# Last layer of a four-layer network: the order of an iteration around VectorE, spreads in one group, mixing in ten steps on a PSUM bank of its own

## The chip, the cores and the metric

The kernel runs on one core of a Trainium2 chip. The metric is the device time of one execution in microseconds (us). The engines are TensorE (PE in the profile, its weight loads PEld), VectorE (DVE), ScalarE (ACT), GpSimd (POOL) and SyncE (SP, which here only issues transfers). Each works through its own queue of instructions, and they wait for one another by semaphores.

## The reference

Four layers work in turn on x, 16 batches of 256 tokens of 128 channels (float32). The change touches the last one. It normalises x, adds an attention scaled per batch by a gate, normalises again, and adds a gated mixing. The attention's sequence runs over the 16 batches: each of the 256 columns attends, for every one of 16 heads of 8 channels, from batch u to the batches 0 to u.

```python
def _L3_attn_ref(x, W_qkv, b_qkv, W_out, b_out):
    T, B, D = x.shape            # 16, 256, 128; H, Dh = 16, 8
    q, k, v = jnp.split(x @ W_qkv + b_qkv, 3, axis=-1)   # to_heads
    scores = jnp.einsum('bhqd,bhkd->bhqk', q, k) / jnp.sqrt(jnp.float32(Dh))
    scores = jnp.where(causal, scores, -jnp.inf)
    context = jnp.einsum('bhqk,bhkd->bhqd', jax.nn.softmax(scores, axis=-1), v)
    return context @ W_out + b_out

def _L3_ffn_ref(x, W_r, W_k, W_v, mu_r, mu_k):
    # x_prev: x one token earlier in its batch, 0 before the first
    xr = mu_r * x + (1.0 - mu_r) * x_prev
    xk = mu_k * x + (1.0 - mu_k) * x_prev
    r = jax.nn.sigmoid(xr @ W_r)
    return r * (jnp.square(jax.nn.relu(xk @ W_k)) @ W_v)

h = _layernorm(x) * (1 + ca) + sa
x = x + ga * _L3_attn_ref(h, ...)
h = _layernorm(x) * (1 + cb) + sb
x = x + gb * _L3_ffn_ref(h, ...)
```

## The kernel before

x lies in SBUF with the channels on the 128 partitions and the 4096 tokens as columns; a batch is 256 columns, a block (two batches) 512. The attention is not done as matrices of queries by keys. For batch u, VectorE multiplies the queries by the keys of all batches up to u, column by column; TensorE sums each head's 8 channels with a matrix of ones, and later spreads the 16 head weights back to 128 channels.

`layer3` (L2287) runs a ring of iterations u = 0 to 18 written out by hand. Iteration u works on four batches at once: u (products), w = u - 1 (softmax), z = u - 2 (weighted values) and a = u - 3 (output projection). The steps are:

- `queries(u)` (L2310): one matmul into the bank ps_q.
- `scores(u, c)` (L2314): VectorE, qk = (ps_q + bias) * keys, for the part c of the earlier batches. `parts` (L2306) makes one part of up to 8 batches, two from u = 8 on.
- `heads(u, c)` (L2323): 8 matmuls with 32 columns of weights, in the trace 16 rows, since a float32 matmul is two passes; the sums S lie in one bank of the pool behind `bank()`.
- `exps(w)` (L2339): VectorE's maximum (top) and subtraction (E), then ScalarE's exponential. `weights(w)` (L2348): VectorE's sum and reciprocal (tot), then the product on GpSimd (E<-E,tot).
- `spread(z, c, half)` (L2355): 4 matmuls (8 rows) into one of two double banks of ps_big. A half is 128 of the 256 tokens.
- `weighted(z, c, half)` (L2364): VectorE's product pv of the spread weights and the values; after the second half a tree of additions on GpSimd, which leaves one or two batches' worth for the projection. The last tree of batch 15 is on VectorE.
- `projected(a)` (L2383): matmuls with the output weights into a bank of `bank()`; `added(a)` (L2390): ScalarE's t (gate and bias), then x += t on GpSimd, and the start of a mixing.

Beside the ring there are generators in the list `sides`; `tick()` advances each by one step, up to its next yield. `keys3(blk)` (L2225) normalises a block and makes its keys and values: blocks 0 to 2 inside layer 2, 3 to 7 in the ring at u = 0, 2, 4, 6 and 8. `mixing3(b0, nb)` (L2239) is the second half of the layer for two batches after every odd one, and for batches 14 and 15 one at a time; it ends with the transfer of x to the output on SP. Both use `normed3` (L2205): the mean by a matmul, ln_xc = x - mean on VectorE, the square on ScalarE, its mean by a matmul, the logarithm and exponential on ScalarE, and the product on GpSimd. Layer 2 calls `keys3` and `normed3` too.

Inside the ring `strict_all` is set, so that every instruction of TensorE, VectorE, ScalarE and GpSimd stays in the order in which the program issues it. Nearly all of them go through the helpers at L219 (VectorE, ScalarE, GpSimd) and L265 (matmuls), and so have those lines in the profile; tiles tell them apart. PSUM has 8 banks: four for ps_big, one for ps_q, three in rotation for `bank()`, which serves heads, projections, keys and mixings (all ps_one in the profile).

## Time and profile before

| | us |
|---|---|
| median of 3 runs | 2811.61 (2802.94 to 2819.47) |
| the profiled execution | 2822.73 |
| its span, first to last instruction | 2821.0 |
| last layer's attention: first product qk (iteration 0) | at 2597.4 |
| first row of iteration 16 (top of batch 15) | at 2768.1 |
| last addition on GpSimd | 2815.3 to 2816.0 |

In the span TensorE is busy for 2574.2 us (91%), VectorE 1856.5 (66%), ScalarE 1590.8 (56%) and GpSimd 1255.8 (45%). The last layer takes about 224 us of the 2821.0; from 2597.35 to 2821.0 TensorE is busy for 171.8 us, VectorE 125.1, GpSimd 112.4 and ScalarE 93.2. These times come from one profiled execution. A row of the timeline gives the start, the length, the engine, the line, the operation with output and inputs, and in brackets how long the engine had been idle before it and what ended the wait. PEclk is the clock that was granted to TensorE, as a share of full speed.

### The profile page before, as it was taken

The page shows a single profiled execution, that of the slowest core. Times are in us where ns is not written, and L with a number is a line of the kernel's source. Part 1 is how long each engine was busy: PE and PEld are TensorE (multiplying, and loading weights), DVE is VectorE, ACT ScalarE, POOL GpSimd, SP SyncE. Part 2 cuts the span into 40 slices and gives each one's busy share as a digit, 9 for nine tenths or more (in the row PEclk, how much of TensorE's full clock was granted, in tenths as well). Part 3 has the DMA queues.
Part 4 walks back from the last instruction along what each step waited for, and adds up shares of the span by engine and source line. Part 5 has one row for each costly group of instructions (what it writes and reads, how often), then busy time and mean ns, then how long its engine had stood idle before and what let it go on. Part 6 is the DMA issues. An engine that isn't in the chain of part 4 may idle for free.

```text
span 2821.0 us, 49133 instructions
## 1 busy us (share of the span) xinstructions
PE 2574.2 (91%) x17190; PEld 1694.3 (60%) x17190; DVE 1856.5 (66%) x4449; ACT 1590.8 (56%) x4166; POOL 1255.8 (45%) x1105
## 2 busy tenths in 40 slices
PE   7999999989799999999999888889889999999886
PEld 4566566656588677777666545558645555443443
DVE  6777767787654467666666777773467885654664
ACT  4666666666544566666665466665435555532533
POOL 5767776876413553334444300142565442000555
PEclk9999999999999999999999999999989999999988
DMA  9240000000177200000000122327623231221000
GB/s 333 33 41 1 7 10 1 11 26 5 38 216 216 88 16 3 1 1 1 1 31 16 49 89 81 98 75 215 202 76 109 86 92 47 79 82 56 8 8 16
DMA packets 119286, 181.04 MB, mean 64 GB/s; under 512 B 18096, under 2 KB 81008, under 8 KB 116736
## 3 DMA queue, kind: packets, MB, share of 16 engines
q1 hardware_dynamic: 97360, 148.51, 18.4%
q0 software_dynamic: 8432, 17.31, 2.2%
q10 hardware_dynamic: 13248, 12.06, 1.2%
q8 instruction: 138, 2.26, 0.3%
q14 instruction: 108, 0.88, 0.1%
HBM read 120.38 MB, written 60.58 MB: 64 GB/s over the span
## 4 chain that ended last, share of the span: by engine, by line
PE 52%; DVE 21%; ACT 14%; POOL 5%; issue 5%; DMA 2%; SPq 1%; DVEq 0%; ACTq 0%; POOLq 0%
PE ps_one L265 24%; PE ps_big L265 8%; ACT E L219 8%; PE ps_one L268 6%; PE ps_out L265 4%; PE ps_hid L265 4%; PE ps_max L265 4%; DVE m L219 3%; POOL E L219 3%; DVE PT L219 3%; DVE r_t L219 2%; DVE sm_neg L219 2%; ACT r_sq L219 1%; PE ps_exp L265 1%; ACT ln_sq L219 1%
## 5 line engine op out<-in xcount | busy, mean ns | idle before, releaser
L219 POOL TENSOR_TENSOR E<-E,sm_inv 128x1024 f32<-128x1024 f32 (+1 forms) x246 | 412.8, 1688 | 505.1 <-DVE sm_inv L219 483.2
L219 ACT ACTIVATE E<-E,sm_neg 128x256 f32<-128x256 f32 x512 | 252.7, 495 | 194.6 <-DVE sm_neg L1210 194.6
L219 ACT ACTIVATE E<-ps_exp 128x1024 f32<-128x1024 f32 x246 | 226.1, 919 | 165.1 <-PE ps_exp L265 162.1
L219 DVE TENSOR_REDUCE m<-ps_max 128x4 f32<-128x1024 f32 x242 | 263.8, 1090 | 82.6 <-PE ps_max L265 81.2
L268 PEld LDWEIGHTS ps_one<-w_cst,E 128*128 128x128 f32 x1792 | 206.9, 144 | 146.1 <-POOL E L219 86.6
L219 ACT ACTIVATE E<-ps_big,sm_neg 128x128 f32<-128x128 f32 (+1 forms) x512 | 208.9, 422 | 138.1 <-DVE sm_neg L219 114.5
L268 PE MATMUL ps_one<-w_cst,E 128*128 128x128 f32 x1792 | 243.3, 281 | 47.6 <-POOL E L219 30.5
L219 POOL DMA_INDIRECT rows<-list_rows,l_i x128 | 127.8, 999 | 342.8 <-DVE inv L219 158.8
L265 PE MATMUL ps_big<-kT,qT 64*128 64x256 f32 (+1 forms) x2048 | 250.7, 374 | 0.0
L219 DVE COPY PT<-ps_one 128x512 f32<-128x512 f32 x320 | 202.5, 678 | 70.5 <-PE ps_one L268 70.1
L265 PE MATMUL ps_one<-PT,v 128*64 128x256 f32 (+1 forms) x2048 | 223.4, 360 | 3.9 <-ACT v L219 2.1
L265 PEld LDWEIGHTS ps_big<-kT,qT 64*128 64x128 f32 x2048 | 173.9, 189 | 50.9 <-issue 35.4
L219 POOL DMA_INDIRECT list_rows<-done,origin x128 | 122.9, 960 | 173.3 <-ACT s L1098 55.2
L1210 DVE CUSTOM_DVE_ANT_0 E<-ps_big,bias 128x256 f32<-128x256 f32 x512 | 181.6, 419 | 6.7 <-PE ps_big L265 4.8
L265 PEld LDWEIGHTS ps_one<-PT,v 128*64 128x64 f32 x2048 | 130.9, 137 | 82.1 <-DVE sm_neg L1210 17.2
L219 POOL TENSOR_TENSOR r_r<-r_r,r_t 128x512 f32<-128x512 f32 x128 | 163.9, 1280 | 25.8 <-DVE r_t L219 23.7
L265 PE MATMUL ps_max<-q,q 60*128 60x256 f32 (+3 forms) x1008 | 127.6, 331 | 47.6 <-DVE m L219 34.8
L219 DVE TENSOR_TENSOR r_r<-ps_rope,a_cw 128x512 f32<-128x512 f32 x128 | 88.2, 689 | 122.4 <-ACT r_sq L219 115.0
L265 PEld LDWEIGHTS ps_max<-q,q 60*128 60x128 f32 (+1 forms) x1008 | 78.6, 192 | 138.1 <-DVE m L219 74.8
L265 PE MATMUL ps_rope<-w_a_qkv,hb 128*128 128x512 f32 x256 | 139.6, 630 | 17.8 <-DVE sm_inv L219 10.8
L219 POOL TENSOR_TENSOR ln_xc<-ln_xc,ln_sq 128x512 f32<-128x512 f32 (+1 forms) x41 | 51.1, 1246 | 234.3 <-ACT ln_sq L219 234.2
L219 POOL TENSOR_SCALAR_AFFINE_SELECT E<-E 128x512 f32<-128x512 f32 x128 | 83.8, 655 | 157.6 <-ACT E L219 157.3
(354 smaller groups left out, 5838.7 us busy)
## 6 DMA issues: line engine op xcount, KB each, us to landing
q<-parts SPq DMA_DIRECT2D x256, 128.0 KB
rows<-zeros SPq DMA_DIRECT2D x8, 2048.0 KB
share<-comb_rows SPq DMA_DIRECT2D x128, 128.0 KB
parts<-parts SPq DMA_DIRECT2D x14, 1024.0 KB
list_w<-in_f_W SPq DMA_DIRECT2D x46, 257.0 KB
done<-l_o ACTq DMA_DIRECT2D x92, 128.0 KB
f_W<-in_f_W SPq DMA_DIRECT2D x27, 386.0 KB
f_room<-in_f_W SPq DMA_DIRECT2D x19, 386.0 KB
```

Of the source, the lines that this page charges most:

```text
L219: ins = f(*args, **kw)
L265: self.ordered(self.nc.tensor.matmul(out, lhsT, rhs, start=start, stop=stop, **kw))
L268: self.ordered(self.nc.tensor.transpose(out, in_, self.c("ident")))
L1210: nc.vector.tensor_tensor_reduce(e[:, i], S[:, i], bias[g][:, i, off : off + T], 1.0, BIG, ALU.add, ALU.min, neg[:, i : i + 1])
```

## The change

Six things change, all in the last layer.

1. The order in an iteration. Before: spreads of z's first part, exps, scores, then halves of weighted and spread in turn with heads, weights, projection and ticks. After: both halves of weighted z, exps, scores, both spreads of z's second part, tick 1, projection, heads, weights, addition, tick 2, both halves of weighted z's second part, scores of the second part, tick 3, both spreads of w's first part, heads of the second part, queries, tick 4. From iteration 16 on the projection and addition come after weighted's second part, and ticks 1 and 2 are called once more.
2. The two halves of a part's spread are issued together.
3. Keys and mixings in the ring take a single bank, ps_side, and `bank()` keeps two banks. A flag, `side_held`, makes the others let a tick pass while a step's sum waits there for VectorE in a later step. The product on GpSimd in normed3 waits for tick 1 or 2.
4. A mixing of two batches has ten steps. The k product (squared ReLU) comes before r (sigmoid).
5. Batches 14 and 15: the addition to x is one VectorE instruction on the projection's sum, and their bias is added to x by ScalarE at the end of iteration 15. Their mixings have fewer steps, and the product of the normalisation, k's ReLU and square, r's ReLU and additions, and the last addition to x are on VectorE. Batch 15's mixing uses `bank()`, and h1b for the sigmoid's logarithm.
6. The final ticks alternate between tick 1 and tick 2.

```diff
@@ -2202,86 +2202,121 @@
         m = self.mods[3]
         self.act.activation(dst, src, AF.Identity, bias=m[:, 3 * half, b : b + 1], scale=m[:, 3 * half + 1, b : b + 1])
 
-    def normed3(self, src, out):
+    def normed3(self, src, out, bank=None, quick=False):
 
         n = src.shape[-1]
-        ps = self.bank()[:, :n]
+        get = bank or self.bank
+        while bank and self.side_held:
+            yield
+        ps = get()[:, :n]
+        self.side_held = bool(bank)
         self.mm(ps, self.c("mean"), src)
         yield
         xc = self.ln.tile([P, BLK], F32, tag="ln_xc", name="ln_xc")[:, :n]
         self.dve.tensor_sub(xc, src, ps)
+        self.side_held = False
         sq = self.ln.tile([P, BLK], F32, tag="ln_sq", name="ln_sq")[:, :n]
         self.act.activation(sq, xc, AF.Square)
         yield
-        ps = self.bank()[:, :n]
+        while bank and self.side_held:
+            yield
+        ps = get()[:, :n]
         self.mm(ps, self.c("mean"), sq)
-        yield
+        if not bank:
+            yield
         self.act.activation(sq, ps, AF.Ln, bias=self.eps5)
         self.act.activation(sq, sq, AF.Exp, scale=-0.5)
-        self.gps.tensor_mul(xc, xc, sq)
+        if quick:
+            self.dve.tensor_mul(xc, xc, sq)
+        else:
+            if bank:
+                yield
+                while self.phase not in (1, 2):
+                    yield
+            self.gps.tensor_mul(xc, xc, sq)
         out.append(xc)
         yield
 
-    def keys3(self, blk):
+    def keys3(self, blk, bank=None):
 
         out = []
-        yield from self.normed3(self.x[:, blk * BLK : (blk + 1) * BLK], out)
+        yield from self.normed3(self.x[:, blk * BLK : (blk + 1) * BLK], out, bank)
         h = self.h3[blk] = self.l3.tile([P, BLK], F32, tag="h3", name="h3", bufs=3)
         for i in range(2):
             self.shifted(h[:, i * T : (i + 1) * T], out[0][:, i * T : (i + 1) * T], 2 * blk + i, 0)
         yield
         for n, (dst, k) in enumerate(((self.k3, "a3_bk"), (self.v3, "a3_bv"))):
-            ps = self.bank()
+            while bank and self.side_held:
+                yield
+            ps = (bank or self.bank)()
             self.mm(ps, self.w3[:, (n + 1) * P : (n + 2) * P], h)
-            yield
+            if not bank:
+                yield
             self.act.activation(dst[:, 2 * blk : 2 * blk + 2, :].rearrange("p b t -> p (b t)"), ps, AF.Identity, bias=self.v(k))
-
-    def mixing3(self, b0, nb):
+            if bank and n == 0:
+                yield
+
+    def mixing3(self, b0, nb, bank):
 
         two, W = self.two3, nb * T
+        quick = nb == 1
         x = self.x[:, b0 * T : (b0 + nb) * T]
-        if nb == 2:
-            yield
-            yield
-        out = []
-        yield from self.normed3(x, out)
-
         h = two.tile([P, 2, T + 1], F32, tag="h3f", name="h3f")
         self.gps.memset(h[:, :, 0:1], 0.0)
+        if not quick:
+            yield
+        out = []
+        yield from self.normed3(x, out, bank, quick)
         for i in range(nb):
             self.shifted(h[:, i, 1:], out[0][:, i * T : (i + 1) * T], b0 + i, 1)
         yield
 
         def mixed(n):
-            ps = self.bank()[:, :W]
+            ps = bank()[:, :W]
             o = ps.rearrange("p (b t) -> p b t", t=T)
             self.mm(o, self.mix[2 * n], h[:, :nb, 1:], start=True, stop=False)
             self.mm(o, self.mix[2 * n + 1], h[:, :nb, :T], start=False, stop=True)
             return ps
 
+        r = two.tile([P, BLK], F32, tag="r3", name="r3")[:, :W]
+        k = two.tile([P, BLK], F32, tag="kr3", name="kr3")[:, :W]
+        l = self.h1[:, :W] if b0 < B - 1 else self.h1b[:, :W]
+        while self.side_held:
+            yield
+        ps = mixed(1)
+        if quick:
+            self.dve.tensor_scalar(k, ps, 0.0, None, ALU.max)
+            self.dve.tensor_mul(k, k, k)
+        else:
+            self.act.activation(k, ps, AF.Relu)
+            self.act.activation(k, k, AF.Square)
+        yield
+        while self.side_held:
+            yield
         ps = mixed(0)
-        yield
-
-        r = two.tile([P, BLK], F32, tag="r3", name="r3")[:, :W]
-        l = self.h1[:, :W]
         self.act.activation(l, ps, AF.Abs)
-        self.act.activation(r, ps, AF.Relu, scale=-1.0)
+        if quick:
+            self.dve.tensor_scalar(r, ps, -1.0, 0.0, ALU.mult, ALU.max)
+        else:
+            self.act.activation(r, ps, AF.Relu, scale=-1.0)
         self.act.activation(l, l, AF.Exp, scale=-1.0)
         self.act.activation(l, l, AF.Ln, bias=self.one)
-        self.gps.tensor_add(r, r, l)
-        ps = mixed(1)
-        yield
-        k = two.tile([P, BLK], F32, tag="kr3", name="kr3")[:, :W]
-        self.act.activation(k, ps, AF.Relu)
-        self.act.activation(k, k, AF.Square)
+        (self.dve if quick else self.gps).tensor_add(r, r, l)
+        if not quick:
+            yield
+        while self.side_held:
+            yield
+        ps = bank()[:, :W]
+        self.side_held = not quick
+        self.mm(ps, self.wv3, k)
         self.act.activation(r, r, AF.Exp, scale=-1.0)
-        ps = self.bank()[:, :W]
-        self.mm(ps, self.wv3, k)
-        yield
+        if not quick:
+            yield
         for i in range(nb):
             c = slice(i * T, (i + 1) * T)
             self.dve.scalar_tensor_tensor(r[:, c], ps[:, c], self.mods[3][:, 5, b0 + i : b0 + i + 1], r[:, c], ALU.mult, ALU.mult)
-        self.gps.tensor_add(x, x, r)
+        self.side_held = False
+        (self.dve if quick else self.gps).tensor_add(x, x, r)
         self.nc.sync.dma_start(out=self.out[:, b0 * T : (b0 + nb) * T], in_=x)
 
     def layer3(self):
@@ -2290,13 +2325,20 @@
         with ExitStack() as ctx:
             self.ps_big = self.pool("ps_big", 2, PSUM, ctx=ctx)
             self.ps_q = self.pool("ps_q", 1, PSUM, ctx=ctx)
-            self.ps_one = self.pool("ps_three", 3, PSUM, ctx=ctx)
+            self.ps_one = self.pool("ps_three", 2, PSUM, ctx=ctx)
+            ps_side = self.pool("ps_side", 1, PSUM, ctx=ctx)
+            self.side_held, self.phase = False, 0
             two = self.two3 = self.ln = self.pool("a3_two", 2, ctx=ctx)
             C = 32
             U = [{} for _ in range(B)]
             sides = []
 
-            def tick():
+            def side():
+                ps = ps_side.tile([P, BLK], F32, tag="side", name="ps_side")
+                return ps
+
+            def tick(phase=0):
+                self.phase = phase
                 for g in list(sides):
                     try:
                         next(g)
@@ -2388,16 +2430,18 @@
                     self.mm(d["A"], self.wo3, p, start=k == 0, stop=k == len(P_) - 1)
 
             def added(u):
-                t = two.tile([P, T], F32, tag="t3", name="t3")
-                self.act.activation(t, U[u]["A"], AF.Identity, bias=self.go3[:, u : u + 1], scale=m[:, 2, u : u + 1])
                 xb = self.x[:, u * T : (u + 1) * T]
-                self.gps.tensor_add(xb, xb, t)
+                if u >= B - 2:
+                    self.dve.scalar_tensor_tensor(xb, U[u]["A"], m[:, 2, u : u + 1], xb, ALU.mult, ALU.add)
+                else:
+                    t = two.tile([P, T], F32, tag="t3", name="t3")
+                    self.act.activation(t, U[u]["A"], AF.Identity, bias=self.go3[:, u : u + 1], scale=m[:, 2, u : u + 1])
+                    self.gps.tensor_add(xb, xb, t)
                 U[u] = None
                 if u >= B - 2:
-                    sides.append(self.mixing3(u, 1))
+                    sides.append(self.mixing3(u, 1, side if u == B - 2 else self.bank))
                 elif u % 2:
-                    sides.append(self.mixing3(u - 1, 2))
-
+                    sides.append(self.mixing3(u - 1, 2, side))
 
 
             self.strict = self.strict_all = True
@@ -2407,49 +2451,48 @@
                 w, z, a = u - 1, u - 2, u - 3
                 b = u // 2 + 3
                 if u % 2 == 0 and b < NBLK:
-                    made[b] = self.keys3(b)
+                    made[b] = self.keys3(b, side)
                     sides.append(made[b])
+                on_u, on_w, on_z, on_a = (0 <= i < B for i in (u, w, z, a))
+                two_u, two_z = on_u and u >= 8, on_z and z >= 8
                 if u == B + 2:
                     projected(a)
                     added(a)
                     break
-                on_u, on_w, on_z, on_a = (0 <= i < B for i in (u, w, z, a))
-                two_u, two_z = on_u and u >= 8, on_z and z >= 8
                 if on_z:
-                    spread(z, 0, 0)
-                    spread(z, 0, 1)
+                    weighted(z, 0, 0)
+                    weighted(z, 0, 1)
                 if on_w:
                     exps(w)
                 if on_u:
                     scores(u, 0)
-                tick()
-                if on_z:
-                    weighted(z, 0, 0)
                 if two_z:
                     spread(z, 1, 0)
+                    spread(z, 1, 1)
+                tick(1)
+                if on_a and u < B:
+                    projected(a)
                 if on_u:
                     heads(u, 0)
                 if on_w:
                     weights(w)
-                if on_a:
+                if on_a and u < B:
+                    added(a)
+                tick(2)
+                if two_z:
+                    weighted(z, 1, 0)
+                    weighted(z, 1, 1)
+                if on_a and u >= B:
                     projected(a)
-                if on_z:
-                    weighted(z, 0, 1)
-                if two_z:
-                    spread(z, 1, 1)
-                tick()
+                    added(a)
                 if two_u:
                     scores(u, 1)
-                if two_z:
-                    weighted(z, 1, 0)
-                    tick()
+                tick(3)
+                if on_w:
+                    spread(w, 0, 0)
+                    spread(w, 0, 1)
                 if two_u:
                     heads(u, 1)
-                if two_z:
-                    weighted(z, 1, 1)
-                if on_a:
-                    added(a)
-                tick()
                 if u + 1 < B:
                     g = made.pop((u + 1) // 2, None)
                     if g in sides:
@@ -2457,9 +2500,18 @@
                             pass
                         sides.remove(g)
                     queries(u + 1)
-                tick()
+                if u == B - 1:
+                    for i in (B - 2, B - 1):
+                        xb = self.x[:, i * T : (i + 1) * T]
+                        self.act.activation(xb, xb, AF.Identity, bias=self.go3[:, i : i + 1])
+                tick(4)
+                if u >= B:
+                    tick(1)
+                    tick(2)
+            n = 0
             while sides:
-                tick()
+                n += 1
+                tick(n % 2 + 1)
             self.strict = self.strict_all = False
```

More of the change, by code (lines that the diff above doesn't have):

```diff
@@ L2233, in keys3 @@
         for n, (dst, k) in enumerate(((self.k3, "a3_bk"), (self.v3, "a3_bv"))):
-            ps = self.bank()
+            while bank and self.side_held:
+                yield
+            ps = (bank or self.bank)()
             self.mm(ps, self.w3[:, (n + 1) * P : (n + 2) * P], h)
-            yield
+            if not bank:
+                yield
             self.act.activation(dst[:, 2 * blk : 2 * blk + 2, :].rearrange("p b t -> p (b t)"), ps, AF.Identity, bias=self.v(k))
-    def mixing3(self, b0, nb):
+            if bank and n == 0:
+                yield
+    def mixing3(self, b0, nb, bank):
         two, W = self.two3, nb * T
+        quick = nb == 1
         x = self.x[:, b0 * T : (b0 + nb) * T]
-        if nb == 2:
-            yield
+        h = two.tile([P, 2, T + 1], F32, tag="h3f", name="h3f")
+        self.gps.memset(h[:, :, 0:1], 0.0)
+        if not quick:
             yield
         out = []
-        yield from self.normed3(x, out)
-        h = two.tile([P, 2, T + 1], F32, tag="h3f", name="h3f")
-        self.gps.memset(h[:, :, 0:1], 0.0)
+        yield from self.normed3(x, out, bank, quick)
         for i in range(nb):
```

## The prediction

> **What bounds the kernel now.** The change touches only the last layer (keys3 and normed3 called without a bank, as layer 2 does, issue what they issued), so I read that layer alone. First, the table of busy time by stage. I cut it where the first product of an even batch starts (row qk<-ps_q), so a line is two iterations, then the end.
>
> ```profile
> core 0: us, PE busy (x) PEld busy (x) DVE busy (x) ACT busy (x) POOL busy (x), PEclk, DMA share, GB/s
> 2622.33:2636.05 13.72, 11.96 (x92) 6.12 (x93) 9.09 (x17) 7.07 (x14) 5.62 (x7) 1.00 0.00 1
> 2636.05:2655.74 19.69, 17.17 (x102) 8.02 (x103) 12.49 (x18) 12.85 (x24) 12.17 (x13) 1.00 0.04 14
> 2655.74:2677.54 21.80, 18.72 (x134) 8.80 (x134) 15.66 (x20) 13.07 (x24) 14.70 (x13) 1.00 0.04 13
> 2677.54:2704.33 26.79, 20.78 (x170) 11.52 (x174) 17.74 (x24) 9.88 (x18) 13.44 (x14) 0.94 0.03 10
> 2704.33:2735.40 31.07, 25.28 (x174) 13.28 (x166) 20.39 (x25) 9.09 (x16) 15.84 (x16) 0.84 0.03 9
> 2735.40:2768.09 32.69, 25.44 (x156) 12.98 (x150) 21.89 (x22) 8.88 (x16) 18.02 (x17) 0.84 0.03 9
> 2768.09:2796.80 28.71, 21.06 (x100) 11.20 (x100) 16.16 (x18) 9.49 (x18) 20.87 (x18) 0.88 0.02 9
> 2796.80:2821.00 24.20, 12.10 (x40) 7.13 (x40) 2.59 (x6) 13.45 (x32) 7.56 (x11) 0.89 0.07 23
> ```
>
> No engine fills a late pair: in the pair of batches 12 and 13 (31.07 us) VectorE works 20.39, and part of TensorE's 25.28 is at a lower clock (0.84). The list of waits says whom VectorE waits for, always TensorE: for the queries (qk), for the mixing's last product (r), and for pv.
>
> ```profile
> DVE qk L219 <- PE ps_q L265: 29.3, 11, 6.1
> DVE r L219 <- PE ps_one L265: 29.2, 7, 6.6
> DVE pv L219 <- PE ps_one L265: 17.9, 6, 6.0
> ```
>
> The timeline of iteration 12 shows why: engines run in program order, and a mixing step that is not ready holds the attention behind it.
>
> ```profile
> 2707.48 3.78 PE L265 MATMUL ps_one<-h3f,mix 128*128 128x512 f32 x4 [2.78 <-ACT h3f L219]
> ...
> 2714.20 3.25 PE L265 MATMUL ps_one<-pv,w_a_o 128*128 128x256 f32 x8
> ...
> 2717.56 1.55 DVE L219 TENSOR_TENSOR pv<-ps_big,v 128x640 f32<-128x640 f32 x2 [5.97 <-PE ps_one L265]
> 2718.12 1.99 PE L265 MATMUL ps_one<-h3f,mix 128*128 128x512 f32 x4
> ...
> 2722.69 0.88 DVE L219 SCALAR_TENSOR_TENSOR r<-ps_one,mod,r 128x256 f32<-128x256 f32 x2 [3.57 <-PE ps_one L265]
> ...
> 2731.26 0.92 PE L265 MATMUL ps_big<-E,w_cst 32*128 32x192 f32 x8
> ...
> 2734.69 1.05 PE L265 MATMUL ps_big<-E,w_cst 32*128 32x224 f32 x16
> ```
>
> TensorE waits 2.78 us for h3f, then runs the four mixing passes in 3.78 us where the same group later takes 1.99. The projection is slow too (3.25; 1.99 at 2729.34). The second spread comes behind all this, and VectorE loses 5.97 and 3.57 us.
>
> By the Trainium skill (TensorE: Matmul & The Clock Gate, section Part 1) an idle window of about 3.4 us halves the clock until a busy one has passed. Here 2.78 us of idle was enough to see it, so the measured wait decides; by the page's figure such a slow stretch needs 0.6 us more idle, and the sum below stays.
>
> **The change part by part.**
>
> *Order and spread.* Both halves of a part's spread run as one group: 1.05 us for 16 matmuls (224 columns) against 0.92 for each group of 8 (192). Eight second parts save about 0.8 each on TensorE, beside VectorE. In the new order VectorE does, without a gap by intent: weighted first part, exps, scores, weights, weighted second part, scores second part. I follow iteration 13 by start-to-start steps: weighted four times 0.9 = 3.5; exps 1.1; two scores of 2.0 (rows 2.07); weights 0.84 + 0.3; sum 9.75. Iteration 12: 3.35 + 1.1 + 3.75 + 1.1, plus the mixing's r (two of 0.4) and ln_xc (0.6): 10.7. Together 20.4, the busy time of the table.
>
> Covers: heads of the second part (0.96) lie behind scores, but the next weighted products (1.8) hide them. The exponential (0.55, ScalarE) is hidden by scores (2.0). The product by the inverse total (POOL, 1.0 to 1.1) and the spread (1.0) are hidden in two-part batches by weighted (1.8) and scores (2.0). In batches below 8 nothing hides them: recip, POOL 0.4 to 0.7, half of the spread (0.5 of the 1.05) and three hand-overs, an estimate of 1.4 to 1.8 us of stall each, in place of today's wait for the queries (1.65 to 4.35 in these iterations).
>
> *Mixing in ten steps, own bank.* The same 7 us of TensorE per pair (two means 1.1, four mixed products twice 1.95, wv 1.1) are placed so that each finds its operand ready. This removes the 2.78 and 5.97 us waits, and the low clock with them. It adds one wait: at tick 3 of an even iteration the next mixing's mean takes the single bank only after r of the one before, and r stands on VectorE behind scores of the second part. TensorE's spread, heads and queries queue behind that mean, and ln_xc of tick 4 waits for it: 0.1 + 1.1 + 0.1, then 0.4 for the spread: 1.7 us per pair. With another 1 us per pair of semaphore gaps (0.02 to 0.1 each between the chain's pieces):
> - pair 12/13: 20.4 + 1.7 + 1 = 23.1; taken 23.5. TensorE at full clock needs 3.8 spread, 3.6 heads, 3.9 projection, 1.3 queries, 6.9 mixing = 19.5, no bound. Gain 7.6.
> - pair 14/15: 21.9 + 1.7 + 1 = 24.6; gain 8.
> - pair 10/11: 17.7 + 2.7 = 20.4, TensorE 20.8 less 1.4 of spread; taken 21, gain 5.8.
> - pair 8/9: TensorE's 18.7 at clock 1.00 binds; taken 19.3, gain 2.5.
> - batches 4 to 7: TensorE 29.1 of 33.4; taken 31.4, gain 2. Bounds: up to 4 down to -3 (the uncovered stall).
> - batches 0 to 3 (25 us, latency of two key blocks): one key product fewer ahead of the queries, but spread and weights now wait in turn; taken 0, within 3 either way.
>
> *The end*, from the start of iteration 16 (2768.1) to the last addition's end (2816.0), 47.9 us. Steps in the new order, in us after the start: weighted 14 to 2.1; exps to 3.5; ACT 4.1; weights 15 to 5.5; weighted 14 second part to 7.5. On POOL the tree of 14 (3.15) ends at 5.3, mixing 10/11's addition follows ScalarE's chain (to 8.9), then the product for 15 (10.1), the second tree (13.2) and x of 13 (13.9). Only then the mean of mixing 12/13 runs (15.1), and its ln_xc stands on VectorE ahead of weighted 15: VectorE idles from 8.3 to 15.2. Weighted 15 ends at 18.2, its second part at 21.7, its tree of two additions (2.97 today) at 24.6, added 14 (0.48 for ACT 0.56 and POOL 0.73) at 25.1. Steps of 12/13 and of 14 now alternate on one bank ahead of projected 15, which runs at 34 to 36; added 15 ends at 36.6, where x of 15 ends at 31.3 today. The last mixing takes 14 (today 16.6): POOL's 0.72 become VectorE 0.41 three times, r and k overlap. Sum 50.6, 2.7 worse. My gaps of 0.1 add up over some 50 hand-overs, so between 6 worse and 9 better (VectorE's busy 16.2 plus the tail alone); I take 0. The SP queue carries the same nine output transfers, the last still at the end (5 us from the last addition to the span's end). The two bias additions on ScalarE (0.55 each) replace two of its t operations.
>
> The Trainium skill (SBUF — State Buffer, section SBUF: two separate sides) speaks against the last part: a VectorE operation with two SBUF inputs and a GpSimd one exclude each other for a whole instruction. One row agrees: pv<-pv 128x512 took 1707 ns on VectorE beside POOL's ln_xc (1.26), the larger 128x1024 1224. By the rule two or three of the quick operations wait up to 1.27 each, some 3 us, where the bare rows give 0; it lies inside the bounds above.
>
> **The sum.** 7.6 + 8 + 5.8 + 2.5 + 2 + 0 + 0 = 26 us. The profiled execution took 2822.7 us (span 2821.0), 11 above the median of 2811.6, so I take the 26 off the median: 2785.6, or 0.9% less.
>
> **Rivals.**
> - *VectorE's floor is reached and the end gains.* Pairs 8 to 15 at busy time plus 1: 16.7 (but TensorE 18.7), 18.7, 21.4, 22.9: gains 3, 8, 9.7, 9.8; batches 4 to 7 give 4, the end 5: 40 us, 2772. For it: heads, exponential and spread all have cover. Against: the r and mean coupling, POOL's order.
> - *The single bank paces the ring.* Each mixing step waits for the bank's last reader, and TensorE in order passes that to the attention; pairs 10 to 15 gain 3 each, the end loses 2: about 10 with batches 4 to 9, 2801. For it: today's three banks rotate and still the steps stall.
> - *Slower: the mixings pile up behind the attention.* Mixing, keys and the next mixing share one bank, and whoever finds it held lets its tick pass; a mixing that needs more than the ten ticks (two iterations have eight) falls back, and what is left runs after iteration 17, where nothing hides it. A full mixing there costs its chain, an estimate of 18 us (mean to x of 12/13 took 21 today, 2787.0 to 2808.0, with some 3 of attention inside), and 4 of half clock (two groups of mixing passes at 3.78 for 1.99). One left over costs 22, and the change still wins 4; two cost 44 against 26: 18 slower, 2830. It decides at two full mixings in the sides list when iteration 17 ends. Against: POOL's and ScalarE's work per pair (18.0, 9.1) leaves room, and ten ticks come to 2.5 iterations.
>
> **How the numbers follow.** Forecast 0.60 (gains of 18 to 36 us), floor 0.16, bank 0.14, slower 0.10. About 0.5% (14 us) is what a measurement of this kernel can tell from no change. The first two are faster by more, 0.76; the bank case (0.4%) is the same, 0.14; slower 0.10. The range goes from 2768, 4 us past the floor case, to 2812, where the bank case's gain has gone altogether; the slower case and the edges stay out.
>
> **What would show it.** Right: pairs of 21 to 25 us from batch 10 on; VectorE's waits for r and pv below 10 us in all; clock near 1.00 from 2677 on; spread rows of 16 only. ln_xc waits for ps_side in even iterations about 1.2. Wrong: pairs above 28, a long wait of TensorE for VectorE's r, or more than 51 us from iteration 16 to the last addition.

## The result, and the profile after

The changed kernel takes 2831.62 us (median of 5, 2826.60 to 2839.57) against 2813.62 (median of 5, 2802.94 to 2820.15): 1.0052 times as long, 95% interval 1.0032 to 1.0072. The forecast was 2785.6, that is faster, so it was wrong in sign, and the result lies above its upper end, 2812.

The profiled execution took 2839.57 us (span 2837.9). The last layer begins at 2606.51, 9.2 us later than in the trace of before, although all instructions ahead of it are the same; in the runs below that start lies between 2586.9 and 2628. So I compare lengths inside the layer, in three stretches: from the first product qk to that of batch 10 (stretch 1, iterations 0 to 9); from there to the maximum (top) of batch 15 (stretch 2); and from there to the last addition (the end).

| us | stretch 1 | stretch 2 | end | layer |
|---|---|---|---|---|
| before | 80.2 | 90.6 | 47.9 | 218.7 |
| after | 95.0 | 76.9 | 56.1 | 228.0 |

The change did what it was to do in stretch 2 (-13.7), and lost 14.8 before it and 8.2 behind it: +9.3 in the traces. The ratio is worth some 14.6; what is missing lies ahead of the layer or in the spread of single traces and can't be placed. In the new order the maximum of batch 15 comes behind batch 14's first weighted product (2.3 us), so stretch 2 holds a little more work than before. Counted as the prediction counts, up to the first row of iteration 16, the pairs 10 to 15 gained 15.9 and the end lost 10.5.

The table of busy time by stage of the kernel after, two batches a line from batch 4 on, the last two lines from iteration 16 to the end of the span (columns: window, length, busy time of each engine with its instructions, granted clock, DMA):

```profile
core 0: us, PE busy (x) PEld busy (x) DVE busy (x) ACT busy (x) POOL busy (x), PEclk, DMA share, GB/s
2631.57:2648.33 16.76, 12.42 (x88) 5.96 (x88) 9.74 (x18) 9.29 (x17) 6.89 (x10) 1.00 0.00 1
2648.33:2672.23 23.90, 18.58 (x100) 8.22 (x101) 13.35 (x20) 11.71 (x22) 11.15 (x13) 1.00 0.03 12
2672.23:2701.50 29.27, 22.17 (x130) 9.72 (x128) 15.00 (x22) 13.64 (x25) 15.87 (x15) 0.83 0.03 10
2701.50:2726.51 25.01, 20.66 (x162) 11.21 (x162) 18.26 (x24) 9.57 (x17) 14.19 (x16) 0.93 0.03 11
2726.51:2751.61 25.10, 21.06 (x164) 11.45 (x162) 20.79 (x25) 9.21 (x16) 16.83 (x17) 0.93 0.03 12
2751.61:2776.12 24.51, 19.84 (x141) 10.73 (x140) 19.74 (x20) 9.04 (x16) 15.91 (x15) 0.86 0.03 12
2776.12:2808.00 31.88, 22.02 (x100) 10.93 (x100) 15.52 (x19) 10.49 (x19) 18.20 (x15) 0.84 0.02 8
2808.00:2837.90 29.90, 16.67 (x42) 9.28 (x40) 8.36 (x19) 9.87 (x21) 2.57 (x3) 0.79 0.05 19
```

The pair 12/13 fell from 31.07 to 25.10, 10/11 from 26.79 to 25.01; but 4/5 rose from 13.72 to 16.76, 6/7 from 19.69 to 23.90 and 8/9 from 21.80 to 29.27, the last with the clock at 0.83. Up to iteration 16 VectorE's busy time hardly moved; its waits did. VectorE's waits in the last layer of the kernel after (who waits for whom: us in total, times, longest):

```profile
DVE ln_xc L219 <- PE ps_side L265: 28.3, 10, 9.0
DVE pv L219 <- PE ps_big L265: 22.3, 10, 4.9
DVE pv L219 <- PE ps_one L265: 11.9, 4, 5.2
```

Of the waits shown of before, r for the mixing's product went from 29.2 to 3.7 and the queries from 29.3 to 3.2. In their place stand ln_xc, behind the new bank, and pv, now for the spread. Iteration 12 shows the part that worked:

```profile
2727.77 1.98 PE L265 MATMUL ps_side<-h3f,mix 128*128 128x512 f32 x4
...
2729.59 1.89 PE L265 MATMUL ps_one<-pv,w_a_o 128*128 128x256 f32 x8
...
2731.59 1.56 DVE L219 TENSOR_TENSOR pv<-ps_big,v 128x640 f32<-128x640 f32 x2 [1.56 <-PE ps_one L265]
...
2735.80 1.30 PE L265 MATMUL ps_side<-x,w_cst 128*128 128x512 f32 x2 [2.37 <-DVE r L219]
...
2737.14 0.69 DVE L219 TENSOR_TENSOR ln_xc<-x,ps_side 128x512 f32<-128x512 f32 x1 [1.48 <-PE ps_side L265]
```

The mixed product finds its operand and takes 1.98 (3.78 before), the projection 1.89 (3.25 before), pv waits 1.56 (5.97 before). The foretold coupling of the mean behind r is there too: TensorE idles 2.37 us, VectorE 1.48. Iteration 8 shows the part that did not:

```profile
2677.18 2.48 PE L265 MATMUL ps_side<-h3f,mix 128*128 128x512 f32 x4 [2.61 <-ACT h3f L219]
...
2680.34 2.08 PE L265 MATMUL ps_side<-ln_sq,w_cst 128*128 128x512 f32 x2 [0.69 <-ACT kr L219]
...
2683.29 2.04 PE L265 MATMUL ps_side<-x,w_cst 128*128 128x512 f32 x2 [0.87 <-ACT ln_sq L219]
2685.26 2.10 PE L265 MATMUL ps_big<-E,w_cst 32*128 32x256 f32 x16
2685.37 0.69 DVE L219 TENSOR_TENSOR ln_xc<-x,ps_side 128x512 f32<-128x512 f32 x1 [8.96 <-PE ps_side L265]
```

Three generators (a mixing, a block of keys, the next mixing) hand the one bank to one another. Each passes it on only when ScalarE has read it (kr, then ln_sq), TensorE stands in order behind each hand-over, and from the second of these rows on all runs at half clock (2.08 for a mean that elsewhere takes 1.12). The spread comes last, and VectorE has idled 8.96 us.

### The profile page after: what moved, and what is told of

Same layout as the page of the kernel before. It is cut to its first block, busy times and chain, and to the rows that moved or that the text cites. A ratio compares the mean times of both kernels' runs of the same rounds, so it can differ in the third digit from the quotient of the medians.

```text
span 2837.9 us, 49104 instructions
## 1 busy us (share of the span) xinstructions
PE 2583.8 (91%) x17190; PEld 1696.0 (60%) x17190; DVE 1866.2 (66%) x4463; ACT 1590.3 (56%) x4160; POOL 1249.9 (44%) x1097
## 4 chain that ended last, share of the span: by engine, by line
PE 53%; DVE 20%; ACT 13%; POOL 5%; issue 5%; DMA 2%; SPq 1%; DVEq 0%; ACTq 0%; POOLq 0%
PE ps_one L265 22%; PE ps_big L265 8%; ACT E L219 8%; PE ps_one L268 6%; PE ps_out L265 4%; PE ps_max L265 4%; PE ps_hid L265 4%; DVE m L219 3%; POOL E L219 3%; DVE PT L219 2%; DVE r_t L219 2%; PE ps_side L265 2%; DVE sm_neg L219 2%; PE ps_exp L265 2%; ACT r_sq L219 1%
## 5 line engine op out<-in xcount | busy, mean ns | idle before, releaser
L219 DVE COPY PT<-ps_one 128x512 f32<-128x512 f32 x320 | 203.1, 679 | 72.4 <-PE ps_one L268 72.1
L219 POOL DMA_INDIRECT list_rows<-done,origin x128 | 122.9, 960 | 173.2 <-ACT s L1098 54.4
L219 POOL TENSOR_TENSOR ln_xc<-ln_xc,ln_sq 128x512 f32<-128x512 f32 x39 | 49.7, 1273 | 220.7 <-ACT ln_sq L219 220.5
```

The costliest lines, as they stand in the source:

```text
L219: ins = f(*args, **kw)
```

## The experiments

The lengths of stages below are each from one trace. How far one trace can be trusted is seen where code is equal: stretch 1 of before is 80.2, and 80.2, 80.2, 80.0, 79.1 and 82.9 in the five kernels below that leave it alone; the pair 10/11 of before was 26.8 three times and 31.0 once; stretch 1 of after, 95.0, was 98.8 in x3_end, which leaves it alone. So a difference of some 4 us between two traces shows little, one of 13 or 14 much.

**1. The order alone, the steps alone.** x1_order has the new order with the old mixings, banks and last batches; x2_steps has everything but the new order.

```diff
 # x1_order: before, with the iteration of after
-                if on_z: spread(z, 0, 0); spread(z, 0, 1)
+                if on_z: weighted(z, 0, 0); weighted(z, 0, 1)
...
 # x2_steps: after, with the iteration of before
-                if on_z: weighted(z, 0, 0); weighted(z, 0, 1)
+                if on_z: spread(z, 0, 0); spread(z, 0, 1)
...
```

> The ring's new order alone: the steps of keys and mixings, the three rotating banks and the additions of batches 14 and 15 are those of before. First product to first product of batch 10 took 80.2 us before and 95.0 after; that of batch 10 to weighted 14 in iteration 16 98.6 and 74.6; from there to the last addition 47.9 and 58.4 (before: from the maximum of batch 15). Bank theory (keys and mixings pass one bank from hand to hand, and TensorE waits for ScalarE to empty it): the first stretch goes back to 79 to 84, the second stays at 76 to 82, since there the order does the work. Order theory (the uncovered spread of one-part batches and bunched ticks cost the time): the first stretch stays at 92 to 97. The end is 52 to 60 by both, because x of 13 stays behind the second tree of 14.

> The other half alone: the ring's order of before, with the new steps of keys and mixings, their own bank, and batches 14 and 15 on VectorE. Bank theory: the first stretch (80.2 before, 95.0 after) is 90 to 100, the second (98.6 and 74.6) 95 to 105. Order theory: the first stretch is 78 to 82, the second near before's 98. The end (47.9 and 58.4) is 45 to 50 by both, if VectorE's short operations are worth anything.

In both texts 98.6 for the second stretch of before is a slip for 90.6, and 74.6 for after ends earlier than in the table (76.9). Measured, stretch 1, stretch 2, end: x1_order 93.4, 68.5, 51.6; x2_steps 88.9, 83.5, 54.1. The order alone loses 13.2 in stretch 1, as the order theory said, and gains 22.1 in stretch 2, 8 more than the whole change. The steps and the bank alone lose 8.7, near the 90 to 100 of the bank theory, and gain 7.1 in stretch 2, which neither theory had expected; their end is 6.2 longer than before's, not shorter. The losses in stretch 1 don't add up to that of the whole change (14.8). That is what waits in one queue would give; the runs don't show more.

**2. The bank, and the end.** x5_rot takes the bank away: the sides rotate through three, as before; the flag stays. x3_end puts the projection and addition of iterations 16 and 17 back to the ring's place.

```diff
 # x5_rot: after
+            self.ps_one = self.pool("ps_three", 3, PSUM, ctx=ctx)
             def side():
+                return self.bank()
 # x3_end: after
-                if on_a and u < B: projected(a) ... added(a)
+                if on_a: projected(a) ... added(a)
...
-                if on_a and u >= B: projected(a); added(a)
```

> The change with one edit: keys and mixings take the three banks of the other sums in rotation, as before the change, in place of the bank of their own; order and steps stay. Bank theory: the first stretch falls from 95.0 to 80 to 86 us, the clock of batches 8 and 9 (0.83) is 1.00 again, the second stretch stays within 3 of 74.6. Order theory: the first stretch stays at 92 to 97.

> The change with one edit: in iterations 16 and 17 the projection and the addition stand where they stand in all others, behind tick 1 and weights, and no longer behind weighted's second part. If the end's loss comes from that place (weighted 14 waits 3.75 us for projection 13, which frees the one buffer of pv's second part, and x of 13 stands behind a tree of 3.1 us on GpSimd), the end falls from 58.4 to 48 to 53 us. If it comes from the mixings that alternate on one bank ahead of projection 15, it stays at 56 to 60. The stretches ahead of it stay at 95.0 and 74.6.

x5_rot: 86.7, 75.9, 50.3. Against after the bank of its own costs 8.3 in stretch 1, 1.0 in stretch 2 and 5.8 at the end; stretch 1 lies between the two theories, and a loss of 6.5 stays there with the order and the steps. The 1.0 is uncertain: x6_cover and x7_spread below, also without the bank, have 71.2 and 72.1 for stretch 2. x3_end: 98.8, 78.1, 54.4: the end gains 1.7 of the 8.2 (56.6 as the text counts it), so the projection's place there is not what lost most of it.

**3. Cover, or the queue?** Both start from x5_rot. x6_cover puts weights ahead of scores in iterations 0 to 7; x7_spread issues the spread of one-part batches ahead of tick 3, and so ahead of the side steps.

```diff
 # x6_cover
+                    if u < 8: weights(w)
                 if on_u: scores(u, 0)
...
-                if on_w: weights(w)
+                if on_w and u >= 8: weights(w)
 # x7_spread
+                if on_w and not two_z: spread(w, 0, 0); spread(w, 0, 1)
                 tick(3)
-                if on_w: spread(w, 0, 0); spread(w, 0, 1)
+                if on_w and two_z: spread(w, 0, 0); spread(w, 0, 1)
```

> The kernel x5_rot with one edit: in iterations 0 to 7 weights comes ahead of scores, so that the product on GpSimd and the spread lie beside scores (1.0 to 2.3 us). In x5_rot VectorE waited 19.0 us for the spread (pv<-ps_big) in the first stretch of 86.7. Cover theory (the spread is late because its own chain, GpSimd and TensorE, starts late): the wait falls below 8, the stretch to 76 to 81. Queue theory (the spread is late because the steps of keys and mixings stand ahead of it on TensorE): the wait stays at 14 to 20, the stretch at 83 to 89.

> The kernel x5_rot with one edit: as long as no second part is in hand (iterations 1 to 9) the spread stands on TensorE ahead of tick 3, so ahead of that tick's steps of keys and mixings. Queue theory: VectorE's wait for pv falls from 19.0 to 6 to 12 us, and the first stretch from 86.7 to 76 to 82; what stays is the chain of GpSimd and spread, about 1 us in each of eight. Cover theory: the wait stays above 14 and the stretch at 83 to 89. The rest of the layer stays as in x5_rot (75.9 and 50.3).

x6_cover: stretch 1 100.9, 14 worse, against both theories: the exponential now has no cover (VectorE's sum waits 12.6 us for it, 2.4 in x5_rot), and the wait for the spread grew too, from 19.0 to 29.1. x7_spread: 84.2, only 2.5 better, though pv's wait fell from 19.0 to 9.9 us as the queue theory said; the waits for the queries and for the mixing's product (r) grew instead. With the mixings in the queue, moving one step mostly chose who waits.

**4. Without mixings.** n_before and n_after leave out the layer's second half: `mixing3` yields once and stores x.

```diff
     def mixing3(...):
-        two, W = self.two3, nb * T
+        yield
         x = self.x[:, b0 * T : (b0 + nb) * T]
-        ...
         self.nc.sync.dma_start(out=self.out[:, b0 * T : (b0 + nb) * T], in_=x)
```

> The kernel before with the mixings left out (the layer's second half is not computed; x after the attention is what is stored). Key steps, attention and their order stay. Stretch 1 (first product qk to that of batch 10) is 80.2 us with mixings, stretch 2 (from there to the maximum of batch 15) 90.6. Theory 'steps in TensorE's queue': mixings ahead of the attention are what costs in both stretches, so stretch 1 falls to some 72 to 76 (mixings begin with batch 0/1 in iteration 4) and stretch 2 to 66 to 74, near TensorE's and VectorE's work without them. Rival 'order of the attention': the waits of VectorE come from halves of weighted and spread in turn, stretch 2 stays above 80.

> The kernel after with the mixings left out (the layer's second half is not computed). Stretch 1 is 95.0 with mixings, stretch 2 76.9. Theory 'steps in TensorE's queue and one bank': without mixings only the keys stand on the bank, so stretch 1 falls by 10 or more, to 76 to 84, within 6 of n_before, and stretch 2 to 58 to 64. Rival 'order alone': the new order itself has no cover for the spread while a batch has one part (iterations 0 to 9), so stretch 1 stays 10 or more above n_before's, 86 to 92, with VectorE waiting for the spread (pv) as long as before, 19 us or so.

Stretch 1 is 67.3 and 81.4, stretch 2 68.9 and 56.2. Without a single mixing the changed order still loses 14.1 early and gains 12.7 late, so mixings are not the cause of the early loss, and the theory that they are falls. The rival is right in the difference, though stretch 1 of n_after is below its 86. VectorE's first wait in stretch 1, of n_before and of n_after:

```profile
DVE qk L219 <- PE ps_q L265: 22.1, 11, 5.3
```

```profile
DVE pv L219 <- PE ps_big L265: 30.8, 9, 5.2
```

Nine waits for the spread, 3.4 us each, stand in place of eleven for the queries, 2.0 each.

**5. Without keys too.** In z_before and z_after also the key steps of the ring are gone (keys and values from batch 6 on are zeros, later queries read block 2). n7_spread is n_after with the spread ahead of tick 3, as in x7_spread.

```diff
 # z_before, z_after
-                    made[b] = self.keys3(b)
-                    sides.append(made[b])
+                    self.h3[b] = self.h3[2]
```

> The kernel before with neither mixings nor key steps in the ring (keys and values from batch 6 on are zeros, the queries from there use block 2, the layer's second half is not computed). Stretch 1 was 67.3 us without mixings. Theory 'key step ahead of the spread': the keys cost the old order 5 to 10, so 57 to 62. Theory 'bare chain': the same, since it speaks of the difference to z_after.

> The kernel after with neither mixings nor key steps in the ring (same parts left out). Stretch 1 was 81.4 us without mixings, 14.1 above n_before. Theory 'bare chain': recip, GpSimd's product, spread and two hand-overs stand uncovered in each single-part iteration, so the difference to z_before stays at 10 or more and VectorE's wait for the spread at 2.5 to 3.5 us a time. Rival 'key step ahead of the spread': the chain alone is 1.4 to 1.8 us as foretold, so the waits fall to 2 us or less and the difference to below 6.

> n_after (no mixings) with the spread of one-part batches issued ahead of tick 3, that is ahead of the key step. Stretch 1 81.4 in n_after, 67.3 in n_before. Theory 'key step ahead of the spread': 72 to 76, VectorE's wait for the spread falls from 30.8 to below 20. Rival 'bare chain': 78 to 82, the wait goes to the queries or stays.

Stretch 1 is 45.1 in z_before, 59.5 in z_after, 69.8 in n7_spread. The window of z_before, then that of z_after:

```profile
2596.48:2641.58 45.10, 30.60 (x374) 19.42 (x378) 39.30 (x66) 6.75 (x16) 21.55 (x25) 0.92 0.05 19
```

```profile
2592.91:2652.41 59.50, 43.05 (x386) 26.65 (x390) 41.18 (x68) 6.53 (x16) 23.48 (x27) 0.67 0.04 14
```

With nothing beside the attention the old order keeps VectorE busy for 39.30 of 45.10 us and waits 2.3 for queries; the new one idles 18.3. Its first wait, and one iteration of it:

```profile
DVE pv L219 <- PE ps_big L265: 16.1, 9, 2.8
```

```profile
2629.87 0.35 DVE L219 RECIPROCAL tot<-tot 128x32 f32<-128x32 f32 x1
2630.37 0.65 POOL L219 TENSOR_TENSOR E<-E,tot 128x224 f32<-128x224 f32 x1 [1.33 <-DVE tot L219]
...
2631.08 1.90 PE L265 MATMUL ps_big<-E,w_cst 32*128 32x224 f32 x16 [0.56 <-POOL E L219]
...
2633.05 2.09 DVE L219 TENSOR_TENSOR pv<-ps_big,v 128x896 f32<-128x896 f32 x2 [2.83 <-PE ps_big L265]
```

VectorE ends the reciprocal and has nothing until the spread is there; the spread itself runs at half clock (1.90 where before has 1.05), and VectorE's product starts only when all of it has ended (2632.98), not half. Each theory was right by half. The bare chain costs 16.1 / 9 = 1.8 us a time, near the 1.4 to 1.8 foretold and not 2.5 to 3.5; yet the difference is 14.4, not below 6. The key steps cost the old order 67.3 - 45.1 = 22.2 (5 to 10 were expected) and the new one 21.9: the same. So the bare chain's stall comes on top of the wait for the keys' steps, and that wait only changes its name, from queries to spread. With the spread ahead of the key steps (n7_spread) both overlap: pv waits 13.7, and 11.6 of the 14.1 are back. With the mixings (x7_spread) that was not so.

One thing was not taken apart. In these pairs the new order also has the lower clock in stretch 1 (0.85 against 0.93 without mixings, 0.67 against 0.92 without keys), and what part of the 14 us comes from that is open. In the kernels before and after the clock of stretch 1 is 0.91 in both, and it is 14.8 longer all the same.

**6. The order where it has cover.** h1_middle is before, with the new order in iterations 10 to 15 alone, where each batch in `weighted` has two parts. To join the two orders, iteration 9 issues the spread of batch 8 at its end, and iteration 16 leaves out the spread that iteration 15 has issued.

```diff
+                if 10 <= u < B:
+                    weighted(z, 0, 0); weighted(z, 0, 1); exps(w); scores(u, 0)
+                    spread(z, 1, 0); spread(z, 1, 1); tick()
+                    projected(a); heads(u, 0); weights(w); added(a); tick()
+                    weighted(z, 1, 0); weighted(z, 1, 1); scores(u, 1); tick()
+                    spread(w, 0, 0); spread(w, 0, 1); heads(u, 1)
+                    ...  # queries(u + 1); tick()
+                    continue
```

> Before with one edit: iterations 10 to 15 run in the new order, iterations 0 to 9 and 16 to 18 in the old one; steps, three banks and last batches are those of before. If the parts add up, the first stretch is 80 (before 80.2), the second 69 to 74 (x1_order 68.5, before 90.6), the end 46 to 50 (before 47.9), and the time 16 to 22 us below before, a ratio of 0.992 to 0.994. If what the order gains in the middle is only work put off to the end, the end is 60 or more and the ratio 0.998 to 1.002.

2807.25 us (median of 6, 2806.48 to 2816.43) against 2833.50 for before on that chip (median of 11): 0.9918, interval 0.9898 to 0.9939. It beats both kernels. Its stretch 1 is 80.0; stretch 2 follows, two batches a line, then the rest of the span:

```profile
2687.00:2706.90 19.90, 17.79 (x158) 9.88 (x158) 17.86 (x25) 9.65 (x18) 14.52 (x17) 1.00 0.04 14
2706.90:2730.60 23.70, 20.12 (x162) 11.18 (x162) 20.55 (x24) 9.31 (x17) 17.04 (x17) 1.00 0.04 12
2730.60:2753.70 23.10, 19.11 (x144) 10.03 (x144) 19.89 (x20) 8.32 (x15) 17.10 (x15) 1.00 0.03 13
2753.70:2805.30 51.60, 34.43 (x124) 19.15 (x124) 18.84 (x23) 22.63 (x47) 25.44 (x26) 0.83 0.04 16
```

Stretch 2 takes 66.7 us instead of 90.6, at a clock of 1.00, with VectorE busy in 87% of it; the end takes 46.6, so nothing was put off to it. The order does this with the old mixing and rotating banks; neither the ten steps nor the bank were needed.

**7. The end.** p5_last is before with batches 14 and 15 on VectorE as in the change; p5a_mix takes only their mixings over, p5b_add only their additions to x, h2_both is h1_middle with p5a_mix's mixings.

```diff
 # p5_last = both; p5b_add = the first alone; p5a_mix, h2_both = the second alone
+                if u >= B - 2:
+                    self.dve.scalar_tensor_tensor(xb, U[u]["A"], m[:, 2, u : u + 1], xb, ALU.mult, ALU.add)
...
+        quick = nb == 1
+        (self.dve if quick else self.gps).tensor_mul(xc, xc, sq)
...  # r, k and the last addition likewise; with the first, the bias on ScalarE as in the change
```

> Before with one edit: the last two batches on VectorE (the addition on the projection's sum, the bias by ScalarE at the end of iteration 15, and in their mixings the normalisation's product, both ReLUs, the square, and both additions), in the steps of before. By the bare rows three products of 0.72 on GpSimd become 0.41 and two ScalarE operations leave its chain: the end falls from 47.9 to 44 to 47. If VectorE and GpSimd shut each other out for whole instructions there (1707 ns for pv<-pv 128x512 beside a GpSimd product), it stays at 47 to 50.

> The kernel before, with the mixings of batches 14 and 15 on VectorE as in the change, and the additions to x as they were (ScalarE and GpSimd). From the maximum of batch 15 to the last addition: 47.9 before, 54.4 with both edits (p5_last). Theory 'the addition's place': the 6.5 us come from the addition of 14 standing behind weighted 15 and its tree on VectorE, so this run takes 44 to 48. Rival 'VectorE beside GpSimd': they come from the mixings' VectorE operations waiting for GpSimd and for VectorE's queue, so it takes 52 to 55. Layer up to there as in before (80.2 and 90.6).

> The kernel before with only the additions to x of batches 14 and 15 on VectorE (their bias on ScalarE after iteration 15), the mixings as they were. From the maximum of batch 15 to the last addition: 47.9 before (47.1 to VectorE's last r), 54.4 with both, 50.8 with the mixings on VectorE alone. Theory 'the addition stands behind weighted 15 and its tree': 51 to 53 to the last addition on GpSimd. Rival (the mixings' share is all that counts, and p5_last's surplus is run to run): 47 to 49.

> h1_middle (the new order from iteration 10 to 15 alone, 0.9918 of before) and the mixings of batches 14 and 15 on VectorE with the additions to x as they were. If p5a_mix gains at the end (theory 'the addition's place'), the end takes 42 to 46 (45.8 in h1_middle) and the ratio is 0.990 to 0.992. By the rival the end takes 50 to 53 and the ratio is 0.993 to 0.995.

The end, 47.9 before: p5_last 54.4, p5a_mix 50.8, p5b_add 51.9. p5_last is beyond both its cases, and p5a_mix lies between its two. So the additions cost 4.0, as p5b_add's text expected, and the mixings 2.9, for which neither theory had a price; together 6.5. In h2_both the end is 48.0, again between the two cases, against 46.6 in h1_middle (its 45.8 in the text runs to the last addition's start). These 1.4 are no more than before and h1_middle differ by with the same end (1.3). The time is 0.992 of before (0.9901 to 0.9939), no different from h1_middle. So none of these runs shows a gain from VectorE at the end; a loss is clear for both edits together only. The end of the kernel after:

```profile
2786.27 2.09 DVE L219 TENSOR_TENSOR pv<-ps_big,v 128x896 f32<-128x896 f32 x2 [3.75 <-PE ps_one L265]
...
2802.68 2.36 DVE L219 TENSOR_TENSOR pv<-ps_big,v 128x1024 f32<-128x1024 f32 x2 [5.24 <-PE ps_one L265]
...
2808.74 3.41 PE L265 MATMUL ps_side<-h3f,mix 128*128 128x512 f32 x4 [0.51 <-DVE ln_xc L219]
...
2816.76 2.74 PE L265 MATMUL ps_one<-pv,w_a_o 128*128 128x256 f32 x8
2819.55 0.48 DVE L219 SCALAR_TENSOR_TENSOR x<-ps_one,mod,x 128x256 f32<-128x256 f32 x1 [3.37 <-PE ps_one L265]
```

Twice the second part's product stands until a projection (of 13, then of 14) has read the single buffer of that part, 3.75 and 5.24 us with VectorE empty; the mixing that is left and the projection of 15 then run at a lowered clock (3.41 where 1.98 was seen above, 2.74 for 1.89).

## Why the prediction was wrong, point by point

- **Pairs 10 to 15, +21.4 foretold: right in mechanism.** The waits named were removed as told, and the clock of 12/13 rose from 0.84 to 0.93. In the kernel after the pairs gave 15.9: 10/11 1.8 (25.0 us, 21 taken), 12/13 6.0 (25.1, 23.5 taken), 14/15 8.2 as foretold. In h1_middle, where only the order changes, the lines are 19.9, 23.7 and 23.1 for 21, 23.5 and 24.6, at full clock. Of the 7.9 us between the two kernels 5.1 stand in the pair 10/11. x1_order (68.5) against x5_rot (75.9) puts it on the new steps, but x6_cover and x7_spread, with the same steps, have 71.2 and 72.1: by which wait is open.
- **Batches 0 to 9, +4.5 foretold, -14.8 measured: the step that failed.** The stall without cover was seen and its size came out (1.4 to 1.8; 1.8 in z_after), with some luck: the sum takes half of the spread at full clock, and in the rows shown VectorE waits for all of it. But it was put "in place of today's wait for the queries" and so booked at nothing. That wait came from the key steps ahead of the queries in TensorE's queue. They stayed, now ahead of the spread, and z_before, z_after, n_before and n_after show that the two add: 22 us for the keys in either order, and 14 for the order. Even the lower bound named for batches 4 to 7 (-3) was passed: these two pairs lost 7.2. The pair 8/9 lost as much, but without mixings it loses only 1.1 (19.4 and 20.5 in n_before and n_after), and with the new steps and bank in the old order it takes 30.9 (x2_steps): there it is mostly the mixings' steps and their bank.
- **The single bank.** The sum has 1.7 us per late pair for it and nothing for the early ones. It was also a rival (2801), whose mechanism, TensorE passing each wait for the bank to the attention, is what iteration 8 shows; but that was priced by the late pairs, where it costs 1.0. It is dear where three generators are under way, 8.3 in stretch 1, and at the end, 5.8 (x5_rot): 15.1 in all, from one trace against one, more than the 9.3 that the layer lost. Without it the layer took 212.9 in x5_rot against 218.7 before, so by these traces the order's early loss alone would not have made the change slower: 5.8 us of the 26 foretold were left.
- **The end, 0 taken, 2.7 worse by hand, 10.5 worse measured** from iteration 16's first row (58.4 against 47.9), outside the 6 of the bound. The last mixing was sized right (14; 14.5 measured), but batch 15's addition ended 43.9 us after the start, not 36.6. The hand run let the second part of 14 end at 7.5; it ended at 12.2, since the buffer's reader, the projection of 13, was left out; the same recurred for 15, and the sum has no lowered clock, where the two lines of the end had 0.84 and 0.79.
- **The rule on the shared port.** The prediction gave some 3 us by the Trainium skill (SBUF — State Buffer, section SBUF: two separate sides), 0 by the bare rows. In h2_both the rows agree with the rule:

```profile
2800.11 1.27 POOL L219 TENSOR_TENSOR x<-x,r 128x512 f32<-128x512 f32 x1 [4.50 <-DVE r L219]
...
2800.38 1.28 DVE L219 TENSOR_TENSOR ln_xc<-ln_xc,ln_sq 128x256 f32<-128x256 f32 x1 [0.44 <-ACT ln_sq L219]
```

  A product that takes 0.42 alone took 1.28 and ended 0.28 after GpSimd's; the other of this kernel took 0.79. In p5a_mix they took 0.78 and 0.86, and each of the four ended 0.28 or 0.29 after the GpSimd operation beside it. That is 1.2 us in all in h2_both, less than the 3. That this is what the end lost there (1.4) is not shown.
- **The slower rival (2830)** named nearly the time, by luck and not by the way: when batch 15's addition ended at 2820.0, of the mixings ahead of 15's the last steps of 12/13 and the second half of 14 were left, not two whole ones.

## What to carry to other kernels

When a reordering trades one wait for another, ask what causes the old wait: if it is work queued ahead, it stays ahead of whoever comes next, and a chain that lost its cover adds to it. Apply a new order only where it has cover (here from the tenth iteration, 0.8% faster) instead of throughout, and read every stage of the profile by itself. In this kernel a bank of its own for background work was paid for where several generators were under way at once, since a queue that runs in order hands every wait for that bank to the main work.

## What the hardware did that I had not expected

In z_after the granted clock was 0.67 over 59.5 us, although TensorE was never idle for more than 2.3 us at a stretch once the ring was under way. The Trainium skill (TensorE: Matmul & The Clock Gate, section Part 1) speaks of an idle window of about 3.4 us; in z_after the clock fell with no single gap of that length. Nor does the longest gap decide: z_before, with 0.92 over the stretch, had a longer one, and the queries behind it still took 0.70 us, where z_after needs 1.22 at half clock:

```profile
2639.79 0.75 PE L265 MATMUL ps_one<-qk,w_cst 128*32 128x160 f32 x16 [3.01 <-DVE qk L219]
2640.47 0.70 PE L265 MATMUL ps_q<-h,w_a_qkv 128*128 128x256 f32 x2
```

What sets the clock here was not taken apart. What the rows do show is its price for a chain without cover: the work that VectorE waits for takes longer too, the spread of 224 columns 1.90 us instead of 1.05.
